# A graph layer over sorted edges: rows of B loaded per group, a store at the end of its step, and x columns copied on chip for one tile in two groups

## The chip, the cores and the metric

The kernel runs on one core of a Trainium2 chip. The core has five engines, each with its own queue of instructions: TensorE (PE in the profile; PEld is its weight load), VectorE (DVE), ScalarE (ACT), GpSimd (POOL) and SyncE (SP), which issues most DMAs. The metric is the device time of one execution in microseconds. A profile is one execution recorded by the hardware; its span runs from the first instruction to the last.

## The reference

One message-passing layer of a graph network with a residual and a layer norm. There are 12500 nodes with 64 features and 200000 edges with 32 features; the edges are sorted by destination.

```python
msg_in = concatenate([nodes[row], nodes[col], edge_features], axis=-1)
messages = relu(msg_in @ mW1 + mb1) @ mW2 + mb2
aggregated = segment_sum(messages, col, num_segments=12500)
upd_in = concatenate([nodes, aggregated], axis=-1)
y = relu(upd_in @ uW1 + ub1) @ uW2 + ub2
out = layernorm(x + y)
```

Here `row` is an edge's source and `col` its destination. Edges towards low node numbers are much denser than towards high ones, since the destinations are drawn as the square of a uniform number.

## The kernel before, in words

Two tables are made in device memory at the start: A = x times the first 64 rows of mW1 (for sources), and B = x times the next 64 rows plus the bias (for destinations). A tile is 128 edges; there are 1563. A group is 8 tiles (196 groups) and a pair is two groups (98 pairs). The main loop has one step s per group. An even step opens a pair, an odd one closes it.

What happens to group s:

- `gather`: POOL issues one indirect DMA per tile that fetches the 128 source rows of A into an `xg` buffer. Six buffers let POOL run ahead. The first 8 groups fetch rows of x instead.
- `windows`: the destinations of a tile lie in a window of 32 nodes, so 32 rows of B are loaded per tile into `rhs`. SP does it for a whole pair, 16 DMAs, in the even step before the pair (L219 to L227). The rows of an edge's window are picked by a 0/1 matrix in `l`, which `select` (DVE, even steps) makes from the destinations; the edge features are loaded into the same `l` by `load` (SP, behind `select`).
- `edge_part` (PE, L255): destination part and edge part of the hidden layer, one matmul per tile, into PSUM `pc`. It runs in the step before the group's own.
- `node_part` (L277, L278): DVE adds the gathered rows, ACT applies relu, giving `h`.
- `collect` (PE, L290 to L292), one step later: sums `h` over the edges of each of the 32 destinations, transposed, into PSUM `ph` (a single buffer); a bf16 copy of the selection, made on ACT by `counts` (L208), gives the number of edges too.
- `aggregate` (DVE, L304): adds the eight results of a group into `comb`, a table of all nodes on chip, at windows whose start is read from a register.

`comb` holds, per node, the sums in one half and x in the lower partitions of the other half. `copies` uses that: of every fourth group from group 12 on (CG = 4) the last tile isn't gathered. Its 128 source columns of x are copied one by one out of `comb` into `xo`, each at a place read from a register, 32 in each of four steps: 24 by ACT and 8 by DVE (L321, L316, after loads of the places into registers, L317). An extra matmul pair (L258) turns them into the source part.

When all edges of 384 consecutive nodes have been summed, an update is due: `columns` (ACT copies 384 columns, L330), `update` (PE L337 and L338, ACT L340), one step later `residual` (PE L348 and L349, statistics on DVE L353 and L355, square root `sd` on ACT L357), and one step after that `norm` (DVE L363 and L366), which also issues the store of `o` from SP (L368). There are 54 updates: 17 of them after pairs 15 to 60, singly, then one for each pair from 62 on.

The schedule is written by hand: each engine runs its instructions in the order in which this loop emits them (L576 to L611), and waits on semaphores for what it needs. Places in `comb` are known only at run time, so every write to `comb` is ordered against every earlier read of it by another engine, and every read against every earlier write.

The tail of the kernel, for inputs that break the assumptions on the edges, isn't run here.

Of the kernel before, what the change touches and what calls it, by code (L numbers as in the profile page):

```python
# [12 lines left out]
AF = mybir.ActivationFunctionType  # L13
ALU = mybir.AluOpType
AX = mybir.AxisListType
ET = mybir.EngineType

P = 128
N, D, DE, DH = 12500, 64, 32, 128
# [4 lines left out]
NT = -(-E // P)  # L24
SUB = 8
SUP = 16
NSUP = -(-NT // SUP)
NTP = NSUP * SUP
EPAD = NTP * P
NSUB = -(-NT // SUB)  # L30
WIN = 32
# [6 lines left out]
XG = 8  # L38
# [2 lines left out]
EARLY = NCH * P  # L41
GE = 20
BS = 8
CG = 4
CF = 3 * CG
CA = 24
NCT = -(-(NSUB - CF) // CG)
UB = 3
NCOL = (-(-N // P) + UB) * P
# [15 lines left out]
UPD = updates()  # L65
# [3 lines left out]
def gnn_kernel(ctx: ExitStack, tc: tile.TileContext, x1T, x, eT, e_rows, src, src_row, dst, dst_row, wrow, wnext, whalf,  # L69
# [23 lines left out]
    nc = tc.nc  # L93
# [4 lines left out]
    A = dram.tile([NPAD, DH], F32, name="tab_a")  # L98
# [3 lines left out]
    K = len(UPD)  # L102

    src_s = const.tile([P, NT], I32, name="src_s")
    wint = const.tile([1, NTP], I32, name="wint")
# [4 lines left out]
    comb = const.tile([P, 2, NCOL], F32, name="comb")  # L110
# [22 lines left out]
    slot = cps[:, :WIN]  # L133
# [10 lines left out]
    xg = {}  # L144

    def copied(s):

        return s >= CF and s % CG == CG - 1 and len(tiles(s)) == SUB

# [5 lines left out]
    def tiles(s):  # L155
        return range(s * SUB, min((s + 1) * SUB, NT))

    def gather(s):

        if s >= XG or s % 2 == 0:  # L160
            buf = rows.tile([P, SUB, DH], F32, name="xg")
        else:
            buf = xg[s - 1][0]
        d = DH if s >= XG else D
        a = buf.rearrange("p k (b d) -> p (k b) d", d=d)
        if s < XG:
            a = a[:, s % 2 * SUB:(s % 2 + 1) * SUB, :]
        for i, t in enumerate(tiles(s)[:SUB - copied(s)]):
            nc.gpsimd.indirect_dma_start(  # L169
                out=a[:, i, :], out_offset=None, in_=A[:, :] if s >= XG else x[:, :],  # L170
                in_offset=bass.IndirectOffsetOnAxis(ap=src_s[:, t:t + 1], axis=0))
        xg[s] = buf, a

    with tc.tile_pool(name="sup", bufs=2) as sup, tc.tile_pool(name="work", bufs=2) as work, tc.manual_schedule():
# [39 lines left out]
                q = 64 * b + EK  # L214
                nc.sync.dma_start(L[g][q:q + DE], eT[g, b])

        def windows(g):

            nt = min(SUP, NT - g * SUP)  # L219
            r = rhs[g % 2]  # L220
            tab, n = (B0, EARLY - WIN + 1) if g < GE else (B, N)
            _, ws = nc.values_load_multi_w_load_instructions(
                wint[0:1, g * SUP:g * SUP + nt], engines=[ET.SP], min_val=0, max_val=n - 1,
                skip_runtime_bounds_check_because="destinations are node numbers")
            for i in range(nt):
                q = SK + 64 * (i % 2)
                nc.sync.dma_start(r[q:q + WIN, i // 2, :], tab[bass.ds(ws[i], WIN), :])  # L227

        def transpose(s):

# [5 lines left out]
            nc.scalar.copy(xt, pt)  # L236
            xs[s] = xt

        def parts(n):

            if n == SUB:
                return [(slice(None), slice(None))]
            return [(slice(b, b + 1), slice((n - b + 1) // 2)) for b in range(2) if n > b]

        def edge_part(s):

# [14 lines left out]
        def node_part(s):  # L261

            n = len(tiles(s))
            pc = pcs.pop(s)
            h = work.tile([P, 2, SUB // 2, DH], F32, name="h")
            if s < XG:
                xt = xs.pop(s)
                for i in range(n):
                    k, b = divmod(i, 2)
                    q = 64 * b  # L270
                    nc.tensor.matmul(pc[:, b, k, :], xt[q:q + 64, k, :], w1a[q:q + 64], start=False,
                                     stop=i + 2 >= n)
                nc.scalar.activation(h, pc, AF.Relu)
            else:
                a = xg.pop(s)[1].rearrange("p (k b) f -> p b k f", b=2)
                for b, m in parts(n - copied(s)):
                    nc.vector.tensor_tensor(h[:, b, m], pc[:, b, m], a[:, b, m], op=ALU.add)  # L277
                    nc.scalar.activation(h[:, b, m], h[:, b, m], AF.Relu)  # L278
                if copied(s):
                    nc.scalar.activation(h[:, 1, SUB // 2 - 1], pc[:, 1, SUB // 2 - 1], AF.Relu)  # L280
            hs[s] = h
# [24 lines left out]
        def copies(s):  # L306

            t = (s + 2) // CG * CG + CG - 1
            if t < CF or not t < NSUB or not copied(t):
                return  # L310
            n = P // CG
            k = (s + 2) % CG * n
            r = t // CG - CF // CG
            to = xo[t // CG % 2]
            for a, b, e, copy in ((k, k + CA, ET.Activation, nc.scalar.copy),
                                  (k + CA, k + n, ET.DVE, lambda o, i: nc.vector.tensor_tensor(o, i, slot[D:, 0:1], op=ALU.add))):  # L316
                _, v = nc.values_load_multi_w_load_instructions(  # L317
                    srow[r:r + 1, a:b], engines=[e], min_val=0, max_val=N - 1,
                    skip_runtime_bounds_check_because="sources are node numbers")
                for i in range(a, b):  # L320
                    copy(to[D:, i:i + 1], comb[D:, 1, bass.ds(v[i - a], 1)])  # L321

        us = {}

        def columns(u):

            n0 = nc.values_load(usup[0:1, u:u + 1], engines=[ET.PE, ET.SP, ET.Activation], min_val=0, max_val=N - 1,
                                skip_runtime_bounds_check_because="destinations are node numbers")
            xw = work.tile([P, UB * P], F32, name="xw", bufs=1)
            nc.scalar.copy(xw, comb[:, 1, bass.ds(n0, UB * P)])  # L330
            us[u] = (n0, xw)
# [26 lines left out]
            us[u] = (n0, py, mv, sd)  # L358

        def norm(u):  # L360
            n0, py, mv, sd = us.pop(u)
            rs = work.tile([P, UB], F32, name="rs")
            nc.vector.reciprocal(rs, sd)  # L363
            o = work.tile([P, UB, D], F32, name="o")
            for i in range(UB):
                nc.vector.tensor_scalar(o[:, i], py[:, i], mv[:, i, 0:1], rs[:, i:i + 1],  # L366
                                        op0=ALU.subtract, op1=ALU.mult)
            nc.sync.dma_start(out[bass.ds(n0, UB * P), :].rearrange("(c p) d -> p c d", p=P), o)  # L368


# [95 lines left out]
        for k, c in enumerate(range(0, NB, NCH)):  # L466
            chunk_a(c)
            if k == 0:
                chunk_b(0, [B0v, Bv])
            if k == 2:  # L470

                w0 = wint[:, :GE * SUP]
                nc.vector.tensor_scalar(past, w0[:, GE * SUP - 1:], float(EARLY - WIN), None, op0=ALU.is_gt)
                nc.vector.tensor_scalar(w0, w0, float(EARLY - WIN), None, op0=ALU.min)
                windows(0)
            if k == 4:
                relative(0, 8 * SUP)
            if k < 8:
                nc.vector.memset(comb[:P if k < 4 else ONE, k // 4, k % 4 * Q:(k % 4 + 1) * Q], 0.0)
            if k == 9:  # L480
                select(0)
                load(0)
                counts(0)
                for c in range(0, NCOL, XCH):
                    xload(c)
# [81 lines left out]

        due = {SUP // SUB * (UPD[u + 1] if u + 1 < K else NSUP): u for u in range(K)}  # L570
        last = SUP // SUB * NSUP
        transpose(0)
        edge_part(0)
        gathered = XG
# [1 line left out]
        for s in range(last + 3):  # L576
            g, j = divmod(s, SUP // SUB)
            while gathered < NSUB and frees(gathered) < s:
                gather(gathered)
                gathered += 1  # L580
            if s - 2 in due:
                norm(due[s - 2])
            if j == 0 and g + 1 < NSUP:
                windows(g + 1)
            if s < NSUB:
                node_part(s)
            if 1 <= s <= NSUB:
                collect(s - 1)
                aggregate(s - 1)
            if s in due:  # L590
                columns(due[s])
            if j == 0 and g + 1 < NSUP:
                select(g + 1)
                load(g + 1)
                counts(g + 1)
            if j == 1 and g + 2 < NSUP:
                loadd(g + 2)
            if chunks and s >= BS and chunks[0] < NCH + NB * (s + 1 - BS) / (SUP // SUB * (GE - 1) - BS):
                if len(chunks) > 1:
                    columns_of(chunks[1], nc.sync)  # L600
                chunk_b(chunks.pop(0), [Bv])
            copies(s)
            if s + 1 < NSUB:
                if s + 1 < XG:
                    transpose(s + 1)
                edge_part(s + 1)
            if s in due:
                update(due[s], "pt" if s == last else "pu")
            if s - 1 in due:
                residual(due[s - 1], "pt" if s - 1 == last else "pu")  # L610
            rest(s)  # L611


    flag = nc.values_load(flag_i[0:1, 0:1], min_val=0, max_val=2 * EBULK,
# [164 lines left out]
```

## Time and profile before

| | |
|---|---|
| time before, median of 3 runs | 2021.47 us (2020.52 to 2025.77) |
| profiled execution | 2022.05 us |
| its span | 2020.3 us |
| busy: PE, DVE, ACT, POOL | 1436.1, 1065.8, 815.3, 1433.5 us |
| granted TensorE clock, mean | 0.555 of full speed |
| gathers of A | 1454, mean 944 ns |
| single-column copies, ACT and DVE | 4320 and 1440 |
| rows of B loaded | 1563 DMAs of 16 KB |
| stores of updates | 54 of 96 KB |

"Busy" is the time in which an engine executes. In a line of the costliest groups, the numbers after the first bar are busy time in all and mean duration, and those after the second are the idle time of the engine just before, with what ended it ("issue" means nothing the profile shows). In a timeline, a row has start, duration, engine, line, operation, written and read tiles, count, and in brackets the idle time ahead of it and its releaser. Busy times of overlapping instructions are not added twice, so a row's busy time can be less than count times mean.

### The profile page before, as it was taken

To read this page: it belongs to the slowest core of one execution; us is meant where nothing else is said; L and a number is where in the kernel's file an instruction comes from. 1 tells how busy PE (TensorE), PEld (TensorE's weight loads), DVE (VectorE), ACT (ScalarE), POOL (GpSimd) and SP (SyncE) were. 2 spreads that over 40 slices of the span, in tenths; PEclk is the share of its full clock that TensorE was granted. 3 is DMA by queue.
4 is the path that set the end of the run, shared out by engine and by line. 5 is a ranking of instruction groups with operands and counts; after the bars stand their busy time and mean duration, and the time that the engine had idled before them with its cause. 6 is when DMAs were issued, how large, how long until landed. Compare 5 with 4: busy or idle time off the path is not lost.

```text
span 2020.3 us, 43783 instructions
## 1 busy us (share of the span) xinstructions
PE 1436.1 (71%) x7961; PEld 1282.8 (63%) x7961; DVE 1065.8 (53%) x4146; ACT 815.3 (40%) x4890; POOL 1433.5 (71%) x1527
## 2 busy tenths in 40 slices
PE   3578788766667677675776676777677767767767
PEld 3467777656656666565676666666566656656655
DVE  3436676555554555555555555545545545554544
ACT  0122555444434444344444444533433443443431
POOL 7676777777777777777777777777777776666640
PEclk6565555555555555555555555656655655655566
DMA  7744555433333333333333333333333333333330
GB/s 199 207 134 121 149 151 134 121 96 92 96 97 97 97 91 99 102 90 97 99 96 95 101 99 92 101 89 92 93 99 92 92 100 85 85 94 86 85 81 18
DMA packets 243103, 209.33 MB, mean 104 GB/s; under 512 B 79824, under 2 KB 208350, under 8 KB 242432
## 3 DMA queue, kind: packets, MB, share of 16 engines
q1 hardware_dynamic: 178692, 98.71, 18.5%
q0 software_dynamic: 48576, 97.48, 17.9%
q10 hardware_dynamic: 15554, 10.31, 1.8%
q14 instruction: 217, 1.78, 0.3%
q8 instruction: 64, 1.05, 0.2%
HBM read 187.59 MB, written 18.68 MB: 102 GB/s over the span
## 4 chain that ended last, share of the span: by engine, by line
POOL 28%; PE 24%; issue 18%; DMA 10%; DVE 10%; ACT 4%; SPq 3%; ACTq 2%; DVEq 1%; POOLq 0%
POOL xg L169 28%; PE ph L292 9%; DVE comb L304 6%; PE pc L255 6%; DMA l<-in_eT 4%; DMA xg<-tab_a,src_s 4%; PE py L348 2%; ACT xo L321 2%; SPq L227 2%; PE py L349 2%; ACTq L317 1%; PE pu L337 1%; DMA xl<-in_x1T 1%; DVE sel L200 1%; DVE l L196 1%
## 5 line engine op out<-in xcount | busy, mean ns | idle before, releaser
L169 POOL DMA_INDIRECT xg<-tab_a,src_s x1454 | 1372.0, 944 | 492.9 <-issue 410.3
L255 PE MATMUL pc<-rhs,l 64*128 64x128 f32 x3126 | 435.7, 429 | 307.7 <-DMA l<-in_eT 166.3
L292 PEld LDWEIGHTS ph<-sel,h 128*128 128x128 f32 x3126 | 617.7, 302 | 23.2 <-issue 21.9
L292 PE MATMUL ph<-sel,h 128*128 128x32 f32 x3126 | 606.9, 365 | 1.0 <-ACT h L278 1.0
L255 PEld LDWEIGHTS pc<-rhs,l 64*128 64x128 f32 x3126 | 373.5, 316 | 333.6 <-DVE xo L316 114.7
L321 ACT COPY xo<-comb 64x1 f32 x4320 | 456.6, 188 | 180.4 <-issue 109.5
L304 DVE TENSOR_TENSOR comb<-comb,ph 128x64 f32 x1563 | 345.4, 221 | 218.6 <-ACT xo L321 90.6
L277 DVE TENSOR_TENSOR h<-pc,xg 128x1024 f32<-128x1024 f32 (+3 forms) x234 | 226.0, 982 | 365.2 <-DMA xg<-tab_a,src_s 224.4
L278 ACT ACTIVATE h<-h 128x1024 f32<-128x1024 f32 (+3 forms) x234 | 197.2, 862 | 388.1 <-DVE h L277 295.5
L316 DVE TENSOR_TENSOR xo<-comb,cps 64x1 f32<-64x1 f32 x1440 | 156.9, 161 | 59.5 <-DVE comb L304 51.0
L290 PE MATMUL ph<-selb,one 128*128 128x256 bf16 x196 | 76.4, 390 | 131.6 <-DVE comb L304 131.4
L208 ACT CAST selb<-sel 128x512 bf16<-128x512 f32 x98 | 60.4, 616 | 241.9 <-DVE sel L200 230.9
L353 DVE BATCH_NORM_STATS2 st<-py 128x6 f32<-128x64 f32 x162 | 26.7, 220 | 215.4 <-PE py L349 214.9
L290 PEld LDWEIGHTS <-one 128*128 128x128 bf16 x196 | 29.4, 150 | 170.2 <-DVE comb L304 147.3
L337 PE MATMUL pu<-comb,w2u 128*128 x108 | 87.1, 909 | 58.0 <-DVE comb L304 56.3
L196 DVE TENSOR_TENSOR l<-l,cps 128x1024 f32<-128x1024 int32 (+1 forms) x101 | 123.3, 1221 | 3.8 <-DMA rhs<-tab_b 0.2
L348 PE MATMUL py<-ux,xw 128*128 128x64 f32 x324 | 103.2, 421 | 7.0 <-ACT hTu L340 7.0
L357 ACT ACTIVATE sd<-mv,eps 128x3 f32<-128x3 f32 x54 | 16.0, 297 | 221.8 <-DVE mv L355 221.2
L349 PE MATMUL py<-u,hTu 128*128 128x64 f32 x324 | 100.9, 414 | 0.0
L348 PEld LDWEIGHTS py<-ux,xw 128*128 128x128 f32 x324 | 83.9, 318 | 19.6 <-ACT hTu L340 9.5
L349 PEld LDWEIGHTS py<-u,hTu 128*128 128x128 f32 x324 | 86.5, 326 | 0.0
L169 POOL DMA_INDIRECT xg<-in_x,src_s x64 | 60.5, 946 | 21.0 <-issue 18.9
(79 smaller groups left out, 648.1 us busy)
## 6 DMA issues: line engine op xcount, KB each, us to landing
l<-in_dst_row SPq DMA_DIRECT2D x196, 128.0 KB
l<-in_eT SPq DMA_DIRECT2D x196, 128.0 KB
rhs<-tab_b SPq DMA_DIRECT2D x1563, 16.0 KB
xg<-tab_a,src_s POOLq DMA_INDIRECT x1454
tab_b<-tb SPq DMA_DIRECT2D x13, 512.0 KB
tab_a<-tb ACTq DMA_DIRECT2D x12, 512.0 KB
out<-o SPq DMA_DIRECT2D x54, 96.0 KB
comb<-in_x1T SPq DMA_DIRECT2D x6, 520.0 KB
```

Of the source, the lines that this page charges most:

```text
L169: nc.gpsimd.indirect_dma_start(out=a[:, i, :], out_offset=None, in_=A[:, :] if s >= XG else x[:, :], in_offset=bass.IndirectOffsetOnAxis(a ...
L196: nc.vector.tensor_tensor(l[r], l[r].bitcast(I32), node[r].unsqueeze(2).broadcast_to([r.stop - r.start, SUP // 2, P]), op=ALU.is_equal)
L255: nc.tensor.matmul(pc[:, b, k, :], L[g][q:q + 64, m, :], rhs[g % 2][q:q + 64, m, :], start=s >= XG or k == 0, stop=s >= XG and not c)
L277: nc.vector.tensor_tensor(h[:, b, m], pc[:, b, m], a[:, b, m], op=ALU.add)
L278: nc.scalar.activation(h[:, b, m], h[:, b, m], AF.Relu)
L292: nc.tensor.matmul(ph[:, i, 0, :], h[:, i % 2, i // 2, :], S[g][:, k0 + i, :], start=True, stop=True)
L304: nc.vector.tensor_tensor(to, to, ph[:, i], op=ALU.add)
L316: (k + CA, k + n, ET.DVE, lambda o, i: nc.vector.tensor_tensor(o, i, slot[D:, 0:1], op=ALU.add))):
L321: copy(to[D:, i:i + 1], comb[D:, 1, bass.ds(v[i - a], 1)])
L337: nc.tensor.matmul(pu, w2u, comb[:, 0, bass.ds(n0, UB * P)], start=True, stop=False)
L348: nc.tensor.matmul(py[:, i], xw[:, i * P:(i + 1) * P], ux, start=True, stop=False)
L349: nc.tensor.matmul(py[:, i], hT[:, i * P:(i + 1) * P], u2, start=False, stop=True)
```

## The change

- `CG` goes from 4 to 2: of every second group from group 12 on, the last tile has its x columns copied on chip. Its 128 columns are copied in two steps, 64 in each: 48 by ACT and 16 by DVE. ACT's 48 places are loaded by two register loads of 24, and all loads of an engine now stand ahead of its copies.
- `windows` is called in every step for the 8 tiles of group s + 2, not in even steps for 16 tiles.
- An update is due one step later, so its `columns` and `update` fall in an odd step, `residual` in the even step after it and `norm` in the next odd one. `columns` stands ahead of `collect` and `aggregate` of its step.
- The store leaves `norm` and is issued at the end of the same step.
- Gathered rows are laid out in the order of `h`, so the seven gathered tiles of a copied group are added by one instruction and pass relu in one, not two.

```diff
-CG = 4
-CF = 3 * CG
-CA = 24
+CG = 2
+CF = 6 * CG
+CA = 48
...
+            a = buf.rearrange("p (b k) d -> p k b d", b=2)
...
-        def windows(g):
-
-            nt = min(SUP, NT - g * SUP)
+        def windows(s):
+
+            g = s // (SUP // SUB)
+            o = s % (SUP // SUB) * SUB
+            nt = len(tiles(s))
             r = rhs[g % 2]
...
-                nc.sync.dma_start(r[q:q + WIN, i // 2, :], tab[bass.ds(ws[i], WIN), :])
+                nc.sync.dma_start(r[q:q + WIN, (o + i) // 2, :], tab[bass.ds(ws[i], WIN), :])
...
-                for b, m in parts(n - copied(s)):
-                    nc.vector.tensor_tensor(h[:, b, m], pc[:, b, m], a[:, b, m], op=ALU.add)
-                    nc.scalar.activation(h[:, b, m], h[:, b, m], AF.Relu)
+                hf, pf = (t.rearrange("p b k f -> p (b k) f") for t in (h, pc))
+                a = xg.pop(s)[0]
+                for m in parts(n, copied(s)):
+                    nc.vector.tensor_tensor(hf[:, m], pf[:, m], a[:, m], op=ALU.add)
+                    nc.scalar.activation(hf[:, m], hf[:, m], AF.Relu)
...
-            for a, b, e, copy in ((k, k + CA, ET.Activation, nc.scalar.copy),
-                                  (k + CA, k + n, ET.DVE, lambda o, i: nc.vector.tensor_tensor(o, i, slot[D:, 0:1], op=ALU.add))):
+            def by_dve(o, i):
+                nc.vector.tensor_tensor(o, i, slot[D:, 0:1], op=ALU.add)
+
+            parts = []
+            for a, b, e, copy in ((k, k + CA // 2, ET.Activation, nc.scalar.copy),
+                                  (k + CA // 2, k + CA, ET.Activation, nc.scalar.copy),
+                                  (k + CA, k + n, ET.DVE, by_dve)):
                 _, v = nc.values_load_multi_w_load_instructions(
                     srow[r:r + 1, a:b], engines=[e], min_val=0, max_val=N - 1,
                     skip_runtime_bounds_check_because="sources are node numbers")
-                for i in range(a, b):
-                    copy(to[D:, i:i + 1], comb[D:, 1, bass.ds(v[i - a], 1)])
+                parts += [(copy, a + i, v[i]) for i in range(b - a)]
+            for copy, i, v in parts:
+                copy(to[D:, i:i + 1], comb[D:, 1, bass.ds(v, 1)])
...
         def norm(u):
-            n0, py, mv, sd = us.pop(u)
+            n0, py, mv, sd = us[u]
...
+            us[u] = (n0, o)
+
+        def store(u):
+            n0, o = us.pop(u)
             nc.sync.dma_start(out[bass.ds(n0, UB * P), :].rearrange("(c p) d -> p c d", p=P), o)
...
-        due = {SUP // SUB * (UPD[u + 1] if u + 1 < K else NSUP): u for u in range(K)}
-        last = SUP // SUB * NSUP
+        due = {SUP // SUB * (UPD[u + 1] if u + 1 < K else NSUP) + 1: u for u in range(K)}
+        last = SUP // SUB * NSUP + 1
...
             if s - 2 in due:
                 norm(due[s - 2])
-            if j == 0 and g + 1 < NSUP:
-                windows(g + 1)
+            if s + 2 < NSUB:
+                windows(s + 2)
             if s < NSUB:
                 node_part(s)
+            if s in due and s < last:
+                columns(due[s])
             if 1 <= s <= NSUB:
                 collect(s - 1)
                 aggregate(s - 1)
-            if s in due:
-                columns(due[s])
+            if s == NSUB:
+                columns(K - 1)
...
             rest(s)
+            if s - 2 in due:
+                store(due[s - 2])
```

More of the change, by code (lines that the diff above doesn't have):

```diff
@@ L163, in gather @@
             buf = xg[s - 1][0]
-        d = DH if s >= XG else D
-        a = buf.rearrange("p k (b d) -> p (k b) d", d=d)
         if s < XG:
-            a = a[:, s % 2 * SUB:(s % 2 + 1) * SUB, :]
+            a = buf.rearrange("p k (b d) -> p (k b) d", d=D)[:, s % 2 * SUB:(s % 2 + 1) * SUB, :]
+        else:
+            a = buf.rearrange("p (b k) d -> p k b d", b=2)
         for i, t in enumerate(tiles(s)[:SUB - copied(s)]):
             nc.gpsimd.indirect_dma_start(
-                out=a[:, i, :], out_offset=None, in_=A[:, :] if s >= XG else x[:, :],
+                out=a[:, i, :] if s < XG else a[:, i // 2, i % 2, :], out_offset=None, in_=A[:, :] if s >= XG else x[:, :],
                 in_offset=bass.IndirectOffsetOnAxis(ap=src_s[:, t:t + 1], axis=0))
@@ L222, in windows @@
             _, ws = nc.values_load_multi_w_load_instructions(
-                wint[0:1, g * SUP:g * SUP + nt], engines=[ET.SP], min_val=0, max_val=n - 1,
+                wint[0:1, s * SUB:s * SUB + nt], engines=[ET.SP], min_val=0, max_val=n - 1,
                 skip_runtime_bounds_check_because="destinations are node numbers")
@@ L237, in transpose, with parts @@
             xs[s] = xt
-        def parts(n):
+        def parts(n, last=False):
             if n == SUB:
-                return [(slice(None), slice(None))]
-            return [(slice(b, b + 1), slice((n - b + 1) // 2)) for b in range(2) if n > b]
+                return [slice(0, SUB - last)]
+            return [slice(b * SUB // 2, b * SUB // 2 + (n - b + 1) // 2) for b in range(2) if n > b]
         def edge_part(s):
@@ L274, in node_part @@
             else:
-                a = xg.pop(s)[1].rearrange("p (k b) f -> p b k f", b=2)
-                for b, m in parts(n - copied(s)):
-                    nc.vector.tensor_tensor(h[:, b, m], pc[:, b, m], a[:, b, m], op=ALU.add)
-                    nc.scalar.activation(h[:, b, m], h[:, b, m], AF.Relu)
+                hf, pf = (t.rearrange("p b k f -> p (b k) f") for t in (h, pc))
[3 more added lines that the diff above has]
+                    nc.scalar.activation(hf[:, m], hf[:, m], AF.Relu)
                 if copied(s):
@@ L475, in gnn_kernel @@
                 windows(0)
+                windows(1)
             if k == 4:
```

## The prediction

> **What bounds the kernel now.** I read the page, then the windows of the aggregation and of the gathers (how fast the groups of eight tiles go by, stage by stage), then the waits, then the timeline of a few steps. A step is one group; an even step and the odd one after it are a pair (one g of the code, 16 tiles).
>
> ```profile
> L169 POOL DMA_INDIRECT xg<-tab_a,src_s x1454 | 1372.0, 944 | 492.9 <-issue 410.3
> L321 ACT COPY xo<-comb 64x1 f32 x4320 | 456.6, 188 | 180.4 <-issue 109.5
> ```
>
> Each gather is 0.944 us and 0.30 us of issue behind it: one per 1.2475 us. A copy "lasts" 188 ns, but 4320 of them fill 456.6 us, so one comes out every 0.105 us.
>
> The aggregation (L304, eight instructions a group) by stage; columns: stretch, its length, DVE busy and (count), clock, DMA share, GB/s:
>
> ```profile
> 600.00:700.00 100.00, 19.36 (x88) 0.50 0.35 94
> 1100.00:1200.00 100.00, 17.87 (x82) 0.52 0.36 98
> 1500.00:1600.00 100.00, 15.95 (x72) 0.57 0.36 97
> 1700.00:1800.00 100.00, 15.95 (x72) 0.60 0.34 91
> ```
>
> From 400 to 1200 us 658 instructions go by: 9.73 us a step, 19.45 a pair. The gathers of a pair, 15.5 on average, need 15.5 x 1.2475 = 19.34: POOL bounds this stage. From 1300 to 1900 us it is 435: 11.03 a step, 22.07 a pair. There POOL has stopped being the bound (same view of L169, POOL busy):
>
> ```profile
> 1100.00:1200.00 100.00, 75.61 (x81) 0.52 0.36 98
> 1800.00:1900.00 100.00, 66.69 (x72) 0.59 0.32 86
> ```
>
> The waits say what bounds the late stage (first line: SP's own waits; columns: total us, times, longest):
>
> ```profile
> SPq L368 <- DVE o L366: 477.3, 52, 12.6
> PE pc L255 <- DMA l<-in_eT: 166.3, 45, 8.3
> DVE comb L304 <- ACT xo L321: 90.6, 42, 2.7
> ```
>
> A store stands in SP's queue ahead of the next pair's 16 row loads and edge loads, and waits for norm; PE waits for the edges; the norm waits for PE's residual. From pair 62 on every pair has an update (before that, 17 lone ones), so this loop (about 21.5 us) turns every pair. The third line is a second loop, with slack today: aggregation and copies both touch `comb`. One pair at leisure:
>
> ```profile
> 1025.62 2.00 DVE L304 TENSOR_TENSOR comb<-comb,ph 128x64 f32 x8
> 1029.70 0.62 ACT L208 CAST selb<-sel 128x512 bf16<-128x512 f32 x1 [2.83 <-DVE sel L200]
> 1031.41 2.31 ACT L321 COPY xo<-comb 64x1 f32 x22 [1.09 <-issue]
> 1033.90 0.28 ACT L321 COPY xo<-comb 64x1 f32 x2 [0.19 <-issue]
> 1034.22 2.02 DVE L304 TENSOR_TENSOR comb<-comb,ph 128x64 f32 x8
> 1036.27 2.50 ACT L321 COPY xo<-comb 64x1 f32 x24 [0.85 <-DVE comb L304]
> ```
>
> Even step: aggregation, selection on DVE, cast on ACT, then a pause, 24 copies in 2.8 us, and the next aggregation. Odd step: the 24 copies follow the aggregation at once and take 2.50. The pause is the register load:
>
> ```profile
> L317 DVEq TENSOR_LOAD <-srow x180: 593/606/971, 177.0 to 1945.1; - x180
> L317 ACTq TENSOR_LOAD <-srow x180: 1489/1509/2888, 178.9 to 1943.0; - x180
> L327 ACTq TENSOR_LOAD <-usup x54: 277/282/297, 334.7 to 2006.4; - x54
> ```
>
> Minimum, median, maximum ns: one register 0.28 us, eight 0.61, twenty-four 1.51. It grows with the registers.
>
> **What the Trainium skill says.** "Advanced Engine Details and Errata", Sequencer and Instruction Queues: engine instructions are pushed into a queue and wait there for semaphores, control instructions run in the sequencer. "Perfetto Trace Analysis", Identifying Dependency Chains: an instruction that waits for several engines may get an EventSemaphore ahead of it. The cast L208 has one, for DVE; it holds the sequencer, and the load behind it starts at 1029.7, with the cast. In an odd step nothing holds it: the load starts at 1770.0, before the relu ahead of it (1770.55). The trace agrees with both. "DMA: Bandwidth & Descriptors", Latency and other measured facts, gives a tensor_load a floor of about 600 ns; here one register takes 282 ns, and the measurement decides.
>
> **The change, part by part.**
>
> *Gathers.* One tile in 16, not in 32, is copied: 1408 gathers of A for 1454. 46 x 1.2475 = 57.4 us off POOL; its pair becomes 15 x 1.2475 = 18.71.
>
> *SP.* Row loads come eight a step, the edge load stands behind 8 of them, not 16 (0.55 us each), and the store goes to the end of its step, when norm is done. The 21.5 us loop is broken; SP issues 16 x 0.55 for rows, 0.8 + 0.9 for edges and destinations, 0.4 for a store (timeline), and its register loads: about 13 us a pair. What is late next decides: it isn't SP.
>
> *Copies.* ACT makes 48 a step in place of 24, after two loads of 24 registers; DVE 16 for 8. DVE's extra (8 x 0.085 = 0.7 us) lies beside ACT's copies. ACT's doesn't: each aggregation waits for the last copy of the step before (it overwrites what they read), each first copy waits for the aggregation.
> Even step, from aggregation to aggregation: 4.08 to the cast's start (1025.62 to 1029.70); two loads 2 x 1.51 = 3.02; 0.07; copies 2 x 2.50 and a pause of 0.2 as above; 0.03 to DVE: 12.4 (today 8.6, as 1025.62 to 1034.22).
> Odd step: the loads start with the aggregation (2.0) and outlast it: 3.1; copies 5.0; hand-over 0.1: 8.2.
> Pair without update: 20.6, over POOL's 18.71 and over today's 19.45. The second load is what the trace doesn't show: never are two back to back. From below, 0: both in 1.51; then 10.9 + 7.1 = 18.0 and POOL's 18.71 bounds. From above 1.51, one after the other. I take 1.51, since durations grow with the registers and one sequencer does both; even without its fixed part (0.28) it is 1.2.
>
> *Update, moved by one step.* Columns, update and (a step later) residual now lie odd, odd, even. The `sd` of the residual stands on ACT behind the even step's 48 copies, and on DVE the norm stands ahead of the odd step's add. And the columns' copy `xw` now precedes the aggregation, which waits for it, as it overwrites what `xw` reads; it stands behind the odd relu. So in a pair with an update before and in it: copies end 12.4; sd 0.3, rs and three o 1.1 (1758.89 to 1760.28 in the timeline), add 1.08 (seven tiles, from 1.22 for eight): 14.8; relu 0.95, last tile 0.26, xw 0.51 with its hand-overs: aggregation at 16.6, ends 18.65; copies to 23.9. PE's pu and the next collect beside them: 4.75 (1763.55 to 1768.29), done at 23.5. So 24.0 a pair, over today's 22.07. An update alone adds 0.6 in its pair (xw) and 2.3 in the next (norm before add): 2.9.
>
> *The add of a copied group* is one instruction, not two, and so is its relu: saves some 0.1 us, mostly inside slack. PE's 46 extra pairs of matmuls (L258, 0.63 us) lie in PE's slack.
>
> **Sum.** The loop starts at pair 6. Its first aggregation is near 196 us (96 aggregations by 200); steps 10 and 11 already copy: +6, so 202. Pairs 6 to 61: 56 x 20.6 = 1154, with 17 lone updates 49: 1203. Pairs 62 to 97: 34 x 24.0 = 816, the last two, without copies, at about 17: 850. From the last aggregation to the end 12.5 (2007.86 to 2020.3). Span 202 + 1203 + 850 + 12.5 = 2267.5; the profiled run lies 1.8 over its span (2022.05 to 2020.3) and 0.6 over the median: about 2269. Taken: 2270.
>
> **Rivals.**
>
> 1. *Forecast: the aggregation-copy loop becomes the bound.* 2215 to 2330 (second load 1.2 to 1.51, hand-overs of 0.1 either way). For: every term but one is a duration of this trace, and both waits stand in the changed kernel's order of instructions. 0.63.
>
> 2. *Second load nearly hidden.* Pairs without update at 18.71, with update 24.0 - 1.5 = 22.5, a lone update 2.9 less the 0.7 of slack under POOL; 202 + 56 x 18.71 + 17 x 2.2 + 34 x 22.5 + 34 + 12.5 = 2099. For: the loads were put ahead of all copies, so both may overlap other work; against: in even steps nothing is left to overlap. Still slower. 0.14.
>
> 3. *Heavier.* PE at half clock in the update pairs (pu and collect took 6.4 at 1007.68, so 25.2 or more a pair: +40 over 34 pairs), and two more pauses of 0.2 to 0.3 us a pair (+50 over 92): 2330 to 2400. For: the clock is 0.5 in half the stages. 0.14.
>
> 4. *POOL stays the bound: faster.* SP's loop is gone, and ACT keeps up. 202 + 92 x 18.71 + 12.5 = 1936; up to 2015 if the updates hold a little. It decides at 18.71 us a pair: the update pairs would have to be 5.3 us shorter than I walk them, by copies running ahead of the aggregation's wait, or shorter apiece. For: POOL was the bound for most of the run, and ACT's busy share would rise to about 60% only. Against: the 0.105 us is measured and the order is strict. 0.09.
>
> **How the numbers follow.** The time is the first case's. Range: leave out the fourth (0.09), the lower half of the second (0.07) and the top of the third (0.03): 2105 to 2370. No change is within 0.3%, 6 us, what a measurement of this kernel can tell. Faster 0.085, same 0.015, slower 0.90.
>
> **What would show it.** The wait of the aggregation for ACT's copies at the head of the waits, with hundreds of us; POOL waiting for buffers from early on; 12.4 and 8.2 us from aggregation to aggregation; two loads of 1.5 us one after the other; SP's wait for o nearly gone; `sd` starting right behind the 48th copy. I am wrong if POOL keeps one gather per 1.25 us to the end, or if the second load overlaps the first.

## The result, and the profile after

The changed kernel takes 2330.7 us (median of 4 runs, 2327.92 to 2334.4) against 2020.99 us for the kernel before on the same chip: a ratio of 1.1528, with a 95% interval of 1.1503 to 1.1554. The forecast was 2270 us in a range of 2105 to 2370. The profiled execution of the changed kernel took 2329.42 us, with a span of 2327.6 us at a mean granted clock of 0.549.

From the page of the changed kernel, the costliest groups (after the second bar: idle time ahead, and what ended most of it):

```profile
L169 POOL DMA_INDIRECT xg<-tab_a,src_s x1408 | 1328.9, 944 | 838.6 <-issue 379.2
L330 ACT COPY xo<-comb 64x1 f32 x8736 | 909.0, 188 | 481.1 <-issue 348.9
```

There are 46 gathers fewer, each as long as before, but POOL now idles 838.6 us ahead of them, where it idled 492.9. Most of the old idle time was issue (410.3); without issue it is 459.4 us against 82.6. The single-column copies on ACT fill 909.0 us for 456.6. The aggregation by stage, the same view as of before (stretch, length, DVE busy and count, clock, DMA share, GB/s):

```profile
600.00:700.00 100.00, 17.70 (x80) 0.50 0.30 82
1700.00:1800.00 100.00, 14.19 (x64) 0.57 0.28 77
```

Before, 88 and 72 instructions went by in these stretches; now 80 and 64. The whole loop turns more slowly, in both stages. The waits, first those of SP and then of the other engines (total us, times, longest):

```profile
SPq L381 <- DVE o L375: 157.8, 51, 10.8
...
POOL xg L169 <- DVE h L280: 318.1, 74, 9.3
...
DVE rs L372 <- ACT sd L366: 305.9, 54, 7.8
...
DVE comb L307 <- ACT xw L339: 184.2, 53, 7.3
DVE comb L307 <- ACT xo L330: 178.5, 71, 5.7
...
PE pc L257 <- DMA l<-in_eT: 34.6, 44, 1.9
```

What the change set out to remove is gone. The store waits 157.8 us in SP's queue, not 477.3, and PE waits 34.6 us for the edges, not 166.3. In their place DVE waits for ACT in three ways, 668.6 us in all: the aggregation for the copies and for `xw`, and the norm for `sd`. POOL waits for DVE, since buffers come free only when the add (L280) has read them. In the chain of work that ended last, POOL had 28% before and has no share now; ACT has 23%, its register loads 14%, DVE 22%. A pair without an update in the timeline (start, duration, engine, line, operation, count, idle time ahead of it):

```profile
601.67 2.01 DVE L307 TENSOR_TENSOR comb<-comb,ph 128x64 f32 x8 [5.68 <-ACT xo L330]
...
604.82 3.52 ACT L330 COPY xo<-comb 64x1 f32 x34 [2.04 <-issue]
...
608.53 1.49 ACT L330 COPY xo<-comb 64x1 f32 x14 [0.19 <-issue]
...
610.06 2.00 DVE L307 TENSOR_TENSOR comb<-comb,ph 128x64 f32 x8 [1.32 <-ACT xo L330]
...
614.15 0.62 ACT L208 CAST selb<-sel 128x512 bf16<-128x512 f32 x1 [3.04 <-DVE sel L200]
...
617.47 4.83 ACT L330 COPY xo<-comb 64x1 f32 x47 [2.70 <-issue]
...
622.49 0.19 ACT L330 COPY xo<-comb 64x1 f32 x1 [0.19 <-issue]
622.70 0.95 ACT L281 ACTIVATE h<-h 128x896 f32<-128x896 f32 x1
622.71 2.01 DVE L307 TENSOR_TENSOR comb<-comb,ph 128x64 f32 x8 [5.69 <-ACT xo L330]
```

From aggregation to aggregation the odd step takes 8.39 us and the even one 12.65, 21.04 a pair, where POOL's 15 gathers need 18.71. In the even step the 2.70 us ahead of the copies are the rest of two register loads, which begin only with the cast. Their durations (minimum, median, maximum ns) are those of single loads; the second row is that pair of loads alone, the first of which starts at 614.2 and the second at 615.8:

```profile
L325 ACTq TENSOR_LOAD <-srow x364: 1473/1532/2768, 180.0 to 2274.2; - x182
...
L325 ACTq TENSOR_LOAD <-srow x2: 1535/1536/1537, 614.2 to 615.8; - x2
```

A late pair with an update:

```profile
1809.11 2.02 DVE L307 TENSOR_TENSOR comb<-comb,ph 128x64 f32 x8 [0.93 <-PE pc L257]
...
1817.85 3.81 ACT L330 COPY xo<-comb 64x1 f32 x37 [0.19 <-issue]
...
1821.69 0.30 ACT L366 ACTIVATE sd<-mv,eps 128x3 f32<-128x3 f32 x1
1822.02 0.18 DVE L372 RECIPROCAL rs<-sd 128x3 f32<-128x3 f32 x1 [5.85 <-ACT sd L366]
...
1822.99 1.08 DVE L280 TENSOR_TENSOR h<-pc,xg 128x896 f32<-128x896 f32 x1
```

The statistics of the residual were ready at 1816.2, but `sd` starts at 1821.69, when the 48th copy is out. DVE's norm waits 5.85 us for it, and the add, which needs nothing of the norm, waits behind. After the add come relu and `xw`, and the next aggregation starts at 1825.74, 16.63 us after the last.

### The profile page after: what moved, and what is told of

Same layout as the page of the kernel before. It is cut to its first block, busy times and chain, and to the rows that moved or that the text cites. A ratio compares the mean times of both kernels' runs of the same rounds, so it can differ in the third digit from the quotient of the medians.

```text
span 2327.6 us, 56001 instructions
## 1 busy us (share of the span) xinstructions
PE 1410.1 (61%) x8053; PEld 1244.2 (53%) x8053; DVE 1252.8 (54%) x5573; ACT 1258.5 (54%) x9307; POOL 1390.5 (60%) x1481
## 3 DMA queue, kind: packets, MB, share of 16 engines
q8 instruction: 65, 1.06, 0.2%
## 4 chain that ended last, share of the span: by engine, by line
ACT 23%; DVE 22%; issue 18%; PE 16%; ACTq 15%; DMA 4%; DVEq 1%; SPq 1%
ACT xo L330 18%; ACTq L325 14%; DVE comb L307 10%; PE ph L295 6%; DVE l L196 4%; PE pu L346 3%; DVE sel L200 2%; DVE h L280 2%; ACT selb L208 2%; PE pu L347 2%; PE pc L257 2%; ACT h L281 2%; DMA xl<-in_x1T 1%; DMA tab_a<-tb 1%; DVE o L375 1%
## 5 line engine op out<-in xcount | busy, mean ns | idle before, releaser
L169 POOL DMA_INDIRECT xg<-tab_a,src_s x1408 | 1328.9, 944 | 838.6 <-issue 379.2
L330 ACT COPY xo<-comb 64x1 f32 x8736 | 909.0, 188 | 481.1 <-issue 348.9
L307 DVE TENSOR_TENSOR comb<-comb,ph 128x64 f32 x1563 | 346.2, 222 | 530.5 <-ACT xw L339 184.2
L257 PE MATMUL pc<-rhs,l 64*128 64x128 f32 x3126 | 412.8, 416 | 83.4 <-DMA l<-in_eT 34.6
L257 PEld LDWEIGHTS pc<-rhs,l 64*128 64x128 f32 x3126 | 354.6, 304 | 106.2 <-issue 42.2
L319 DVE TENSOR_TENSOR xo<-comb,cps 64x1 f32<-64x1 f32 x2912 | 347.5, 160 | 118.4 <-issue 114.9
L346 PEld LDWEIGHTS pu<-comb,w2u 128*128 128x128 f32 x108 | 27.1, 311 | 447.6 <-DVE comb L307 447.6
L281 ACT ACTIVATE h<-h 128x1024 f32<-128x1024 f32 (+1 forms) x189 | 187.9, 995 | 134.6 <-DVE h L280 128.9
L280 DVE TENSOR_TENSOR h<-pc,xg 128x1024 f32<-128x1024 f32 (+1 forms) x189 | 216.9, 1148 | 40.2 <-issue 13.2
L372 DVE RECIPROCAL rs<-sd 128x3 f32<-128x3 f32 x54 | 9.5, 176 | 305.9 <-ACT sd L366 305.9
L358 PE MATMUL py<-u,hTu 128*128 128x64 f32 x324 | 84.2, 353 | 0.0
L347 PE MATMUL pu<-xw,uz 128*128 128x384 f32 x108 | 79.9, 843 | 0.0
```

The costliest lines, as they stand in the source:

```text
L169: nc.gpsimd.indirect_dma_start(out=a[:, i, :] if s < XG else a[:, i // 2, i % 2, :], out_offset=None, in_=A[:, :] if s >= XG else x[:, :], ...
L257: nc.tensor.matmul(pc[:, b, k, :], L[g][q:q + 64, m, :], rhs[g % 2][q:q + 64, m, :], start=s >= XG or k == 0, stop=s >= XG and not c)
L280: nc.vector.tensor_tensor(hf[:, m], pf[:, m], a[:, m], op=ALU.add)
L281: nc.scalar.activation(hf[:, m], hf[:, m], AF.Relu)
L307: nc.vector.tensor_tensor(to, to, ph[:, i], op=ALU.add)
L330: copy(to[D:, i:i + 1], comb[D:, 1, bass.ds(v, 1)])
```

## The experiments

The theory of the forecast: the chain from aggregation to copies to the next aggregation has become the bound, lengthened by the second register load, and in update pairs by `sd` behind the copies. Its main rivals: the moved update alone, or the loads of rows by SP, are at fault, and more copies would have been harmless. Ratios are to the kernel before on the same chip, with their 95% intervals.

**One part each: the tiles copied.** The first kernel keeps all of the change but the number of copied tiles. The second makes only that part of the change on the kernel before.

```diff
-CG = 2
-CF = 6 * CG
-CA = 48
+CG = 4
+CF = 3 * CG
+CA = 24
...
-            for a, b, e, copy in ((k, k + CA // 2, ET.Activation, nc.scalar.copy),
-                                  (k + CA // 2, k + CA, ET.Activation, nc.scalar.copy),
+            for a, b, e, copy in ((k, k + CA, ET.Activation, nc.scalar.copy),
```

> The whole change but CG, which goes back to 4 (24 copies a step by ACT after one load of 24, 8 by DVE). Copy-loop theory: a pair without update takes 8.6 + 4.7 us in the loop, far under POOL's 19.34, and an update pair about 12.8 + 7 = 19.8, so POOL bounds nearly to the end: 1920 to 1960 us, faster than before. Update theory (the moved update, with xw ahead of the aggregation and norm behind the copies, costs most of the loss): 2150 us or more.

Measured: 1977.36 us, 0.9768 (0.9741 to 0.9796), some 48 us faster than before (2024.97 there). The direction is the theory's, the size is 17 us short of its range. POOL runs at full pace to the last hundred microseconds of its work (windows of the gathers: POOL busy and count, clock, DMA share, GB/s):

```profile
1700.00:1800.00 100.00, 75.61 (x81) 0.60 0.38 98
1900.00:1974.00 74.00, 15.79 (x17) 0.62 0.20 51
```

About 50 us follow its last gather, since pairs 62 to 95 take 20.28 us in the mean, over POOL's 19.34, and the rest of the work has fallen behind the gathers. The gain lies in these pairs, which took 21.62 us before; the 56 pairs ahead of them take as long as before (1044.6 us and 1043.5).

> The kernel before with CG 2 and the two loads of 24, nothing else of the change. Copy-loop theory: 12.6 + 8.4 = 21.0 us a pair without update and some 23.5 with one (SP's loop at 22 is hidden in it): 2220 to 2290 us. Update theory: within 60 us of before, up to 2080.

Measured: 2268.3 us, 1.1204 (1.117 to 1.1237). The tiles copied cost 243 us by themselves, and the wait is the one foretold:

```profile
DVE comb L304 <- ACT xo L327: 556.1, 124, 6.0
```

So the two parts do not add: the rest of the change gains 48 us where ACT has little to copy, and costs about 62 us (2330.7 against 2268.3) where ACT is the bound. Pairs 62 to 95 take 23.48 us in the mean here and 24.64 in the changed kernel, 40 us in all; the other 20 us lie in the stage of the lone updates.

**The second register load.** ACT loads 24 places once and uses them for both halves of its 48 copies, so half of its columns are those of other edges: the kernel makes as many copies, but leaves out half of the places.

```diff
-                                  (k + CA // 2, k + CA, ET.Activation, nc.scalar.copy),
...
                 parts += [(copy, a + i, v[i]) for i in range(b - a)]
+                if e == ET.Activation:
+                    parts += [(copy, b + i, v[i]) for i in range(b - a)]
```

> The changed kernel with one register load of 24 on ACT in place of two; the second 24 copies use the first 24 places again, so half of ACT's columns are those of other edges. Copy-loop theory with loads one after the other: 1.5 us less in each even step, about 1 less in each odd one, so 18.7 a pair without update and 22.5 to 23 with one: 2110 to 2170 us. If the second load overlaps the first: no less than 2310.

Measured: 2139.15 us, 1.0567 (1.0538 to 1.0595), 0.096 of the time before below the changed kernel, or 1.07 us for each of 182 loads. The pause after the cast shrinks from 2.70 to 1.09 us:

```profile
625.53 0.62 ACT L208 CAST selb<-sel 128x512 bf16<-128x512 f32 x1 [3.05 <-DVE sel L200]
627.24 2.21 ACT L331 COPY xo<-comb 64x1 f32 x21 [1.09 <-issue]
```

The even step falls from 12.65 to 11.05 us (621.43 to 632.48), by the 1.6 us from one load's start to the next; in the odd step the aggregation covers more of it. The second load is therefore not hidden, which was the forecast's main uncertain term.

**The residual ahead of the copies.** In the changed kernel `residual` (its matmuls, statistics and `sd`) is called at the end of an even step; here it stands just ahead of `copies`.

```diff
+            if s - 1 in due:
+                residual(due[s - 1], "pt" if s - 1 == last else "pu")
             copies(s)
...
-            if s - 1 in due:
-                residual(due[s - 1], "pt" if s - 1 == last else "pu")
```

> The changed kernel with residual called ahead of copies, so that sd stands on ACT ahead of the even step's 48 copies and the norm's reciprocal needn't wait for them. If the norm behind the copies is on the path as predicted: 2.0 to 2.4 us less for each of 53 updates, 2205 to 2230 us. If PE's residual or the relu behind the copies ends last anyway: 2320 or more.

Measured: 2238.1 us, 1.1041 (1.1007 to 1.1076), 0.0487 below the changed kernel: 98 us, or 1.8 for each update, a little under the 2.0 to 2.4 expected. `sd` is now done ahead of the copies (1719.55), and two late pairs took 23.23 us each. The relu and `xw` still stand between the copies and the aggregation:

```profile
1726.50 1.50 ACT L330 COPY xo<-comb 64x1 f32 x14 [0.19 <-issue]
1728.03 0.95 ACT L281 ACTIVATE h<-h 128x896 f32<-128x896 f32 x1
...
1729.04 0.50 ACT L339 COPY xw<-comb 128x384 f32 x1
```

That is 1.5 us after the last copy, and it is what the edit could not take away. The same edit on the kernel with CG = 4:

> CG 4 with the rest of the change, and residual ahead of copies. The run with CG 4 alone kept POOL at one gather per 1.25 us until 1920 us and then needed 50 us more, since its update pairs took 20 to 20.9 us and work piled up behind POOL. If sd behind the copies is what makes them longer than POOL's 19.34, this ends 20 to 35 us after the last gather: 1940 to 1957 us. If PE's chain of pu and collect holds them instead: 1970 to 1980.

Measured: 1949.42 us, 0.9621 (0.9596 to 0.9645), 28 us below the kernel without it. In both, the residual behind the copies has a price. In the changed kernel it is more than the 62 us that the rest of the change cost: with the residual first, the whole change is faster than the tiles copied alone (1.1041 against 1.1204).

**Copies shifted from ACT to DVE.** If ACT's chain is the bound, DVE might take some of it. 32 copies by each engine, one load each, with the residual first; the same split with the residual where the change put it; and 40 to 24, ACT's in two loads of 20, residual first.

```diff
-CA = 48
+CA = 32
...
-            for a, b, e, copy in ((k, k + CA // 2, ET.Activation, nc.scalar.copy),
-                                  (k + CA // 2, k + CA, ET.Activation, nc.scalar.copy),
+            for a, b, e, copy in ((k, k + CA, ET.Activation, nc.scalar.copy),
```

> The changed kernel (CG 2) with 32 copies a step by ACT and 32 by DVE, one register load of 32 on each, and residual ahead of copies. Copy-loop theory: ACT's loop falls to about 9.7 + 5.6 us a pair; DVE's own queue (aggregation, selection, load, 32 copies of 0.1 to 0.13, add) takes 18.6 to 20.4, next to POOL's 18.71: 1890 to 1990 us, faster than before. If the number of columns per pair costs the time whoever copies them: 2100 or more.

> The same split, 32 and 32 with one load each, with residual where the change put it. sd then stands behind 32 copies and one load, not 48 and two: 10 to 50 us over the run with residual ahead. If DVE's queue is the bound, the two are within 15 us.

> The changed kernel with 40 copies a step by ACT after two loads of 20, 24 by DVE, and residual ahead of copies. Loads cost by register: 2 x 1.27 us; ACT's loop 11.2 + 6.9 = 18.1 a pair, under POOL's 18.71, update pairs about 20: 1910 to 1990 us. If a load costs by instruction (1.5 each), 0.9 more a pair: 1980 to 2060.

Measured: 2314.72 us, 1.1426 (1.1398 to 1.1455); 2257.84 us, 1.1144 (1.1117 to 1.117); 2133.44 us, 1.0531 (1.0506 to 1.0556). All three expectations missed, the second in its sign. With 32 copies DVE is the bound, in the first of these kernels:

```profile
ACT h L281 <- DVE h L280: 583.5, 185, 9.0
```

DVE's copies come one each 0.13 us (4.17 for 32), and its load of 32 registers takes 2162 ns; ahead of the next add both lie in its queue. The forecast's 0.085 us for a copy on DVE was too low. It is the pace of the eight copies that had queued up behind the selection in the trace of before (0.68 us at 1029.64); the eight of the odd step, with no such queue, took 1.07 us there (1036.83), 0.13 each. Why the residual first, a gain in two kernels, is here a loss of 57 us: DVE's timeline of one late pair of the first kernel,

```profile
1711.89 2.02 DVE L307 TENSOR_TENSOR comb<-comb,ph 128x64 f32 x8
...
1716.22 0.30 DVE L363 BATCH_NORM_AGGREGATE mv<-st 128x2 f32<-128x6 f32 x3
1718.86 1.20 DVE L319 TENSOR_TENSOR xo<-comb,cps 64x1 f32<-64x1 f32 x9 [2.34 <-issue]
...
1724.39 1.08 DVE L280 TENSOR_TENSOR h<-pc,xg 128x896 f32<-128x896 f32 x1
```

and of the second, in the same place:

```profile
1707.74 2.01 DVE L307 TENSOR_TENSOR comb<-comb,ph 128x64 f32 x8
...
1712.45 0.42 DVE L319 TENSOR_TENSOR xo<-comb,cps 64x1 f32<-64x1 f32 x3 [0.71 <-issue]
...
1719.18 1.08 DVE L280 TENSOR_TENSOR h<-pc,xg 128x896 f32<-128x896 f32 x1
```

With the residual first, its statistics stand ahead of DVE's register load. The load then starts late, at 1716.35, and is exposed for 2.34 us; in the second kernel it starts at 1709.93, runs beside DVE's queued work and shows 0.71. The other kernel has the statistics to do after its copies, so not all of the difference remains: from the aggregation to the next add it is 12.50 us against 11.44. These 1.06 us are the loss (57 us over 53 updates: 1.08 each).

The third kernel is 105 us faster than the one with 48 copies and the residual first, 0.58 us for each of 182 steps. Eight copies fewer are worth 8 x 0.105 = 0.84 us on ACT, and two loads of 20 registers, 1287 ns each, up to 0.49 more. Less than half of that shows: DVE has become the longer part of the chain that ended last. Its shares by engine (ACTq and DVEq are the engines' own queues, mostly register loads), first with 48 copies, then with 40:

```profile
ACT 25%; issue 20%; ACTq 19%; PE 18%; DVE 14%; DMA 3%; SPq 1%; DVEq 0%
...
DVE 24%; issue 19%; PE 15%; POOL 13%; ACT 9%; DMA 8%; ACTq 7%; DVEq 4%; SPq 0%; POOLq 0%
```

**The copies ahead of the selection.** The load's pause in the even step is there because the cast, for which ACT waits, stands ahead of it. So the copies go ahead of `select`, `load` and `counts`; they need only the aggregation.

```diff
+            copies(s)
             if j == 0 and g + 1 < NSUP:
                 select(g + 1)
...
-            copies(s)
```

To this the second kernel adds that from group 124 on (pair 62, where every pair has an update) only one tile in four groups is copied, and the third the residual ahead of the copies.

```diff
-        return s >= CF and s % CG == CG - 1 and len(tiles(s)) == SUB
+        return s >= CF and s % (CG if s < 124 else 2 * CG) == (CG if s < 124 else 2 * CG) - 1 and len(tiles(s)) == SUB
```

> The changed kernel, CG 2 and 48 copies by ACT after two loads, with copies called ahead of select and counts. The number of instructions is the same; only ACT's loads no longer wait behind the selection and the cast, but run beside the aggregation, in even steps as in odd ones. Copy-loop theory: an even step falls from 12.6 to about 8.4, a pair to 16.9, so POOL's 18.71 bounds pairs without update; a pair with one about 20.4: 1980 to 2030 us, level with before. If ACT's load of 96 copies a pair costs the time wherever it stands: 2280 or more.

> The same, with one copied tile in two groups only up to group 123, and in four groups after it, where every pair has an update. Copies then fill every second late pair; POOL (18.71 a pair, then 19.34) bounds throughout: the last gather near 1880 us and the end at 1900 to 1930 us, faster than before and than CG 4 throughout. If the late pairs stay over POOL's time: 1950 to 1990.

> The same with residual ahead of copies: sd doesn't wait for them. 0 to 15 us less than without, if late pairs are already near POOL's time; more, up to 40, if the norm still held them.

Measured: 3247.6, 3182.32 and 3099.14 us; but on that chip the kernel before took 3252.65 us, not some 2022, so only ratios can be used, and these for that chip alone: 0.9975 (0.9955 to 0.9996), 0.9763 (0.9704 to 0.9823) and 0.9561 (0.9512 to 0.961). The order of the three is the expected one, the absolute times say nothing. In the trace of the first, ACT's copies come out one or two at a time in places, with gaps ahead of them:

```profile
1505.09 0.19 ACT L330 COPY xo<-comb 64x1 f32 x1 [1.18 <-issue]
...
1523.60 4.93 ACT L330 COPY xo<-comb 64x1 f32 x48 [1.62 <-issue]
```

The last row has 48 copies at full pace on the same chip, and a gather took 946 ns there as elsewhere. The gaps lie in the register operations of the copies, one for each copy (FUSED_REGOPS; minimum, median, maximum ns): here, and then in the kernel run on another chip below,

```profile
L330 ACTq FUSED_REGOPS  x8736: 3/46/1394, 260.1 to 3191.3; - x199
...
L330 ACTq FUSED_REGOPS  x7008: 46/46/52, 178.3 to 1849.0; - x195
```

In the first trace 980 of ACT's register operations take over 0.3 us, 681 us in all; some of DVE's and SP's do too. In the second none does. That is part of the lost time; why they take so long on that chip isn't shown. The third kernel was run again on another chip.

> The kernel of the run before once more (copies ahead of select, two of every four late groups without a copied tile, residual ahead of copies), since the kernel before took 3253 us on that chip and ACT's copies came out one by one there. On a chip where the kernel before takes about 2020: pairs up to 61 at POOL's 18.71 us, with ACT's 96 copies and four loads in them, later ones at 19.34, the last gather near 1880, 1895 to 1930 us. If ACT's copies and loads cost the time wherever they stand: 21 us a pair in the first two thirds, 2100 or more.

Measured: 1915.73 us, 0.9455 (0.9434 to 0.9476), against 2026.39 for before there: the fastest of all, 111 us below before. Its timeline of one pair, first DVE's aggregations, then ACT:

```profile
603.38 2.02 DVE L307 TENSOR_TENSOR comb<-comb,ph 128x64 f32 x8 [1.15 <-ACT xo L330]
...
611.81 2.02 DVE L307 TENSOR_TENSOR comb<-comb,ph 128x64 f32 x8
...
620.32 2.01 DVE L307 TENSOR_TENSOR comb<-comb,ph 128x64 f32 x8 [1.78 <-ACT xo L330]
```

```profile
606.84 4.93 ACT L330 COPY xo<-comb 64x1 f32 x48 [2.26 <-issue]
611.80 0.62 ACT L208 CAST selb<-sel 128x512 bf16<-128x512 f32 x1
```

The even step takes 8.43 us, not 12.65: the loads start with the aggregation, and the cast comes after the copies, beside DVE's next work. This pair took 16.94 us; in the mean of 400 to 1200 us, where 687 aggregations went by, it was 18.6, POOL's 18.71 within the reading. The chain has slack, and POOL is the bound again, early and late (windows of the gathers):

```profile
600.00:700.00 100.00, 75.56 (x81) 0.50 0.38 98
...
1700.00:1800.00 100.00, 75.61 (x81) 0.64 0.39 101
```

Before pair 62 the two later edits act at most on the lone updates, so the short even step is the work of the first, the copies ahead of the selection; with that edit alone, many even steps took 8.3 to 8.6 us on the other chip as well. What each of the three edits is worth in time isn't shown: the changed kernel didn't run on the other chip, and what the later two gained there need not hold here.

## Why the prediction was right, and where it was off

**The mechanism.** It is the forecast's. The chain of aggregation and copies turned into the bound, POOL fell idle, and SP's loop went away without gain. Undoing the tiles copied (0.9768), making that part alone (1.1204) and taking out the second load (1.0567) agree with it. *POOL stays the bound* is excluded by POOL's 459.4 us of idle time beyond issue. One sign came out weaker than foretold: the aggregation's wait for the copies has 178.5 us and isn't at the head of the waits, since in pairs with an update `xw` (184.2) and `sd` (305.9) stand behind the copies, and the wait is put down to them. *The second load nearly hidden* is excluded by the loads of 1532 ns in the trace and by the kernel with one load, which gives some 190 us back. "Advanced Engine Details and Errata" of the Trainium skill, Sequencer and Instruction Queues, has control instructions carried out in the sequencer's own code, while engine instructions are queued. It doesn't name register loads; two of them on one engine, one after the other and each at its full length (614.2 and 615.8), agree with that.

**The terms.** By the timeline, the aggregation of group 12 (the first of pair 6) starts at 213.41, that of group 124 (pair 62) at 1453.54, that of group 192 at 2291.40. The profile's span against the sum:

| term | predicted | measured | difference |
|---|---|---|---|
| to the first aggregation of pair 6 | 202 | 213.4 | +11.4 |
| 56 pairs with 17 lone updates | 1203 | 1240.1 | +37.1 |
| 34 pairs with an update | 816 | 837.9 | +21.9 |
| last pairs and end | 46.5 | 36.2 | −10.3 |
| span | 2267.5 | 2327.6 | +60.1 |

- *Start and end* are two slips of counting that nearly cancel. I took the start of group 12 from "96 aggregations by 200"; these end with group 11, and in the trace of before, group 12 starts at 204.95. At the end I counted four steps of the last two pairs, where three lead to the last aggregation.
- *Pair without update*, 12.4 + 8.2 = 20.6: measured 12.65 + 8.39 = 21.04. The 4.08 us to the cast is 4.09 in the trace. From the cast to the first copy it is 3.32 us for 3.09 (two loads of 1.53 and 0.26 of hand-over, where 0.07 was put). Over 56 pairs 0.44 makes 25 us. The other 12 us of this row are the lone updates, (1240.1 − 56 x 21.04) / 17 = 3.6 us each for 2.9. The term that was too small is that of `xw`: the even step that ends with it takes 14.15 us in the mean of the 17, 1.50 over 12.65, where 0.6 was put. `xw` stands behind a relu that starts only after the last copy. Without an update, that relu runs beside the aggregation (622.70 and 622.71 in the timeline above); with one, the aggregation waits for both.
- *Pair with update*, 24.0: measured 24.64 in the mean. The even step was right, 16.6 for 16.63, with `sd`, norm, add, relu and `xw` behind the copies. The odd step was taken as 7.4 and took 7.83 in the pair from 1801.28: its copies start at 1804.14, 0.86 us after the aggregation ended, because the two loads outlast it. The forecast had this in pairs without an update (3.1) and left it out here. In the next pair the odd step took 8.56. There PE's collect took 3.46 us at a granted clock of 0.50 (1.96 us at 0.94 in the pair before), and the aggregation started 0.75 us after the last copy. Of the 34 odd steps, 19 are of this longer kind:

```profile
1825.74 2.01 DVE L307 TENSOR_TENSOR comb<-comb,ph 128x64 f32 x8 [1.66 <-ACT xw L339]
...
1834.30 2.02 DVE L307 TENSOR_TENSOR comb<-comb,ph 128x64 f32 x8 [1.64 <-PE ph L295]
```

So the time landed where the forecast's own range ends and the rival *Heavier* (2330 to 2400) begins. The two reasons that this rival names both show: longer hand-overs, about 25 us, and PE's clock, by an estimate 14 us (19 odd steps, 0.75 each). The loads left out of the odd update step and the relu ahead of a lone `xw`, about a dozen us each by the same reckoning, it doesn't name. All four are additions to the chain, not another mechanism.

**The moved update** was priced for its place in the loop, and the kernel with the residual first gives 1.8 of those microseconds back for each update. That the price depends on the rest of the change wasn't said in the forecast: with few copies the same move is part of a gain. What part of the 48 us gained there is the store and what part the rows wasn't tried.

## What to carry to other kernels

In these traces a register load takes longer with each register that it fills, and two in a row add up. It starts ahead of an instruction that is queued in front of it (601.53 in the changed kernel, its relu at 601.67), but not ahead of the cast, whose wait for DVE holds the queue. Ahead of that wait, loads and copies make an even step of 8.43 us, behind it one of 12.65. When work is moved from the engine that is the bound, walk the strict order of the engine that receives it from one reuse of the shared buffer to the next; ACT's busy share of 54% didn't show that it was the bound. And one part of a change can gain alone and cost beside another, as the moved update and the stores did here (48 us gained, 62 lost): try the parts apart.

## What the runs showed of the hardware

- Register loads grow with their registers and add up: ACT's take 282 ns for one, 1287 for 20, 1532 for 24 and 2019 for 32; DVE's 606 ns for eight, 1129 for 16 and 2162 for 32. Two of 24 in a row take 2 x 1.53 us.
- A single-column copy at a place from a register comes each 0.105 us on ACT and each 0.13 us on DVE, whatever its "mean" of 188 or 160 ns says. Eight on DVE that had queued up behind other work came each 0.085 us.
- One chip ran two of these programs some 60% longer than another (3252.65 and 3099.14 us for 2026.39 and 1915.73), with register operations of up to 1394 ns ahead of ACT's copies, where 52 ns was the longest on another chip. The cause stays open.
